# Denominators of the first batch summed on TensorE for half of the key tiles

## The chip, the cores and the metric

The kernel runs on one core of one Trainium2 chip. The metric is the device time of one execution in microseconds (us). The core has five engines that run their own instruction queues in order and wait for each other by semaphores: TensorE (PE, matrix products into PSUM; its weight loads are shown as PEld), VectorE (DVE), ScalarE (ACT), GpSimd (POOL) and SyncE (SP, which here only issues DMAs). GpSimd also issues DMAs, among them such as add what they move to what lies at the target.

## The reference

For 16 graphs of 1024 nodes with 256 features and a 0/1 adjacency matrix, two layers follow each other. The first is an attention with 8 heads of 32 features, in which queries, keys and values are the same normalized input, and the mask keeps only neighbours:

```
normed = layer_norm(x, gamma1, beta1)
qkv = normed.reshape(b, n, H, HD).transpose(0, 2, 1, 3)
scores = einsum('bhqd,bhkd->bhqk', qkv, qkv) / sqrt(HD)
attn = softmax(where(adj > 0, scores, -inf))
out = einsum('bhqk,bhkd->bhqd', attn, qkv)
x = x + out;  x = x + gelu(layer_norm(x) @ W1 + b1) @ W2 + b2
```

The second layer is a graph attention over the same mask with one score matrix per graph. Both layers get relu(layer_norm(x)) and are added to x. The change concerns only the softmax denominators of the first layer's attention, in the first of the 16 graphs ("batch 0").

## The kernel before, in words

`fast_path` writes one long program for all 16 batches without a loop on the chip. Python generators (`stream_a` to `stream_s`) yield pieces of work with a place, and the piece with the lowest place is written next. So the attention of batch b stands interleaved with the rest of batch b-1 (MLP and second layer). Only batch 0's attention has no such partner: it runs with the loading and normalization of batches 0 and 1 (`prologue`, `norm_stats` L725 to L730, `normalize` L734, L800 and L801 on GpSimd), the conversion of masks (`convert_mask` L591, fed by DMA) and some products of weights (`setup`, L675 to L700). A planner's clock and `defer` place instructions of VectorE and GpSimd some us after the work that they need, and at the end the order of each engine is fixed as written (the loop over `nc.cur_bb.bb.instructions`).

Attention is computed transposed: keys on partitions, queries along the free dimension. One *pass* takes 512 queries (`qh`) and four heads (`g`), so a batch has four passes. A pass walks over eight *tiles* of 128 keys (`kt` 0 to 7). For a tile:

- `scores` (L975) makes the four heads' scores in two PSUM tensors of 2 x 512 columns (`sc0`, `sc1`, here the *first half* and *second half*), each with one buffer. A scores tensor can thus be written only after the one before it has been read.
- The mask is added in one of two ways. TensorE multiplies it by an identity into the first half ahead of the scores (L570, `s<-mk,ident`), and ScalarE takes the exponential straight from PSUM; or VectorE adds it while it reads PSUM (L996), writes the result to SBUF, and ScalarE takes the exponential there in place (L999). In batch 0 the first half has the first way and the second half the second; in the other batches both halves have the second way.
- One tile later `weigh` (L1012) multiplies the exponentials by the values and accumulates in PSUM (`o`).

The denominator is the sum of exponentials over all keys. Sums over tiles are made elementwise, and `total` (L914) sums over partitions at the end of the pass with a product by ones (`den<-acc`). The elementwise sums are made in `acc` (the exponentials of tile 0) by GpSimd's adding DMAs (`add_up`, L1036), which read an exponential tensor from its buffer, in pool `ep` with five buffers. In batch 0 only the even tiles go this way. The odd tiles lie in pool `midp` (three buffers of a whole tile, `odd`), and VectorE adds each to the next one (L1023, `odd<-odd,odd`); `total` then multiplies both sums by ones, 4 products for `acc` and 4 for `odd`.

After that `invert` (L932, `ptds`) and `finish` (L946, `ptos`, then L948 `ot` on VectorE and L952 on GpSimd, the addition into `h`) apply the denominators. PSUM tensors of these and of most other products come from `ps_tile`, three buffers.

Of the kernel before, what the change touches and what calls it, by code (L numbers as in the profile page):

```python
# [9 lines left out]
F32 = mybir.dt.float32  # L10
# [6 lines left out]
P = 128  # L17
# [476 lines left out]
def fast_path(  # L494
# [28 lines left out]
    nc = tc.nc  # L523
    B, N, D = x.shape
    DFF = W1.shape[1]
    H, HD = 8, D // 8
    GH = 4
    NG = H // GH
# [3 lines left out]
    QW = 512  # L532
    NQH = N // QW
# [6 lines left out]
    pool = lambda name, bufs, **kw: ctx.enter_context(tc.tile_pool(name=name, bufs=bufs, **kw))  # L540
# [7 lines left out]
    midp = pool("midp", 3)  # L548
# [4 lines left out]
    smallp = pool("smallp", 3)  # L553
    psc = pool("psc", 1, space=bass.MemoryType.PSUM)
    pso = pool("pso", 1, space=bass.MemoryType.PSUM)
    psm = pool("psm", 3, space=bass.MemoryType.PSUM)

    def ps_tile(shape, name, dtype=F32):
        return psm.tile(shape, dtype, tag="ps", name=name)

# [2 lines left out]
    def matmul(out, lhsT, rhs, start=True, stop=True):  # L565
        if not quarters[0]:
            nc.tensor.matmul(out, lhsT, rhs, start=start, stop=stop)
            return
        for c in range(0, P, HD):
            nc.tensor.matmul(out[c : c + HD], lhsT[:, c : c + HD], rhs, start=start, stop=stop)  # L570
# [33 lines left out]
    ones = const.tile([P, HD], F32, name="ones")  # L604
# [58 lines left out]
    def setup():  # L663
# [8 lines left out]
        for oc in range(DC):  # L672
            pt = ps_tile([P, DC, P], f"p_wT_{oc}")
            for ic in range(DC):
                nc.tensor.transpose(pt[:, ic, :], wl[:, ic, oc * P : (oc + 1) * P], ident)  # L675
            nc.scalar.copy(wT[:, oc, :], pt.rearrange("p c q -> p (c q)"))
# [3 lines left out]
        def product(dst, lhs, rhs, n, name):  # L680

            for oc in range(DC):
                pp = ps_tile([P, n], f"p_{name}_{oc}")
                for kc in range(DC):
                    matmul(
                        pp,
                        lhs[:, kc, oc * P : (oc + 1) * P],
                        rhs[:, kc, :n],
                        start=(kc == 0),
                        stop=(kc == DC - 1),  # L690
                    )
                nc.scalar.copy(dst[:, oc, :], pp)
# [47 lines left out]
    clock = [0.0]  # L740
    deferred = []

    def defer(us, f):
        deferred.append((clock[0] + us, len(deferred), f))

        return clock[0] + us
# [149 lines left out]
    open_sums = [0]  # L896

    def make_turns():
        room = 3 - open_sums[0] - bool(summed or totalled) if open_sums[0] else 100
        while turns and turns[0][0] <= room:  # L900
            n, f = turns.pop(0)
            room -= n
            f()
# [2 lines left out]

    scored, weighed, summed, totalled = [], [], [], []

    def total(b, qh, g, os, accs):

        den = ps_tile([P, QW], f"den_{b}_{g}_{qh}")
        for j in range(GH):
            for acc in accs:
                nc.tensor.matmul(  # L914
                    den[j * HD : (j + 1) * HD, :],
                    ones,
                    acc[j // 2][:, j % 2, :],
                    start=acc is accs[0],
                    stop=acc is accs[-1],
                )  # L920
        ds = tmpp.tile([P, QW], F32, tag="w2", bufs=3, name=f"ds_{b}_{g}_{qh}")
        nc.scalar.copy(ds, den)
        totalled.append((b, qh, g, ds, os))
# [30 lines left out]
    def attention(b, st):  # L954
        va, kT = st["va"], st["kT"]

        def scores(qh, g, kt):
            qs = slice(qh * QW, (qh + 1) * QW)  # L960
            sc = [
                psc.tile([P, 2, QW], F32, tag=f"sc{i}", name=f"s_{b}_{g}_{qh}_{kt}_{i}") for i in range(2)
            ]

            by_pe = 2 if b == 0 else 0
            if by_pe:
                for j in range(by_pe):
                    matmul(
                        sc[j // 2][:, j % 2, :], ident8, st[qh][:, kt // 2, :, kt % 2], start=True, stop=False
                    )  # L970
                clock[0] += 0.45
            for j in range(GH):
                r = slice(j * HD, (j + 1) * HD)
                for c in range(0, P, P // 2):
                    nc.tensor.matmul(  # L975
                        sc[j // 2][c : c + P // 2, j % 2, :],
                        kT[r, g, kt * P + c : kt * P + c + P // 2],
                        kT[r, g, qs],
                        start=j >= by_pe,
                        stop=True,  # L980
                    )
            mb = st[qh][:, kt // 2, :, kt % 2].unsqueeze(1).to_broadcast([P, 2, QW])
            es = []
            if b == 0 and kt % 2:

                odd = midp.tile([P, 2, 2, QW], F32, tag="mid", name=f"odd_{g}_{qh}_{kt}")
            for i in range(2):
                if b == 0 and kt % 2:
                    e = odd[:, i]
                elif kt == 0:  # L990
                    e = accp.tile([P, 2, QW], F32, tag=f"acc{i}", name=f"acc_{b}_{g}_{qh}_{i}")
                else:
                    e = ep.tile([P, 2, QW], F32, tag="e", name=f"e_{b}_{g}_{qh}_{kt}_{i}")
                masked = sc[i]
                if 2 * i >= by_pe:
                    nc.vector.tensor_tensor(e, masked, mb, op=ALU.add)  # L996
                    masked = e
                es.append(e)
                weights = lambda e=e, masked=masked: nc.scalar.activation(e, masked, AF.Exp, scale=SCALE)  # L999
                if i == 0:  # L1000
                    weights()
            return es, weights

        acc = {}


        def weigh(qh, g, kt, es):
            if kt == 0:
                acc[g, qh] = pso.tile([P, QW], F32, tag="o", name=f"o_{b}_{g}_{qh}")
            o = acc[g, qh]  # L1010
            for j in range(GH):
                nc.tensor.matmul(  # L1012
                    o[j * HD : (j + 1) * HD, :],
                    va[:, kt, (g * GH + j) * HD : (g * GH + j + 1) * HD],
                    es[j // 2][:, j % 2, :],
                    start=(kt == 0),
                    stop=(kt == NT - 1),
                )
            if b == 0 and kt % 2:

                if kt > 1:
                    for n, (e, w) in enumerate(zip(es, odds[g, qh])):
                        defer(1.0 + 2.5 * n, lambda e=e, w=w: nc.vector.tensor_add(e, e, w))  # L1023
                odds[g, qh] = es
            if kt == NT - 1:
                c = tmpp.tile([P, QW], F32, tag="w2", bufs=3, name=f"os_{b}_{g}_{qh}")
                nc.vector.tensor_copy(c, o)
                weighed.append((b, qh, g, c, [s[g, qh] for s in (sums, odds) if s]))

        sums, odds = {}, {}  # L1030


        def add_up(qh, g, kt, e, i):
            if b == 0 and kt % 2:
                return
            nc.gpsimd.dma_start(sums[g, qh][i], e, accum_op=ALU.add)  # L1036

        units = [(qh, g, kt) for qh in range(NQH) for g in range(NG) for kt in range(NT)]
        for u in units:
            make_turns()  # L1040
            es, rest_of_weights = scores(*u)
            go_on()
            rest_of_weights()
            qh, g, kt = u
            if kt == 0:
                sums[g, qh] = es
            else:
                for i in range(2):
                    defer(2.0 + 1.5 * i, lambda u=u, e=es[i], i=i: add_up(*u, e, i))
            scored.append((weigh, (*u, es)))  # L1050
            yield

    def go_on():
        was_weighed, was_summed, was_totalled = weighed[:], summed[:], totalled[:]
        for l in (weighed, summed, totalled):
            l.clear()
        if scored:
            f, args = scored.pop()
            f(*args)
        summed.extend(was_weighed)  # L1060
        for args in was_summed:
            total(*args)
        for args in was_totalled:
            invert(*args)
        clock[0] += 2.0
# [354 lines left out]
    def stream_a():  # L1420
        for b in range(B):
            yield from spread(attention(b, states[b]), 32, b, b + 1)
        yield from spread(close_attention(), 4, B, B + .1)
# [55 lines left out]
    while any(p is not None for p in places):  # L1479
        i = min((p, i) for i, p in enumerate(places) if p is not None)[1]  # L1480
# [17 lines left out]
    last = {}  # L1498
# [74 lines left out]
```

## Time and profile before

| what | value |
|---|---|
| median of three runs | 3482.66 us (3480.26 to 3485.44) |
| profiled execution, span from first to last instruction | 3468.1 us |
| median of the runs above that span | 14.6 us |
| batch 0's four passes, first scores to the first scores of the next batch | about 25 to 151 us |
| TensorE busy | 3420.8 us, 99% |
| VectorE busy | 2746.2 us, 79% |
| ScalarE busy | 1858.1 us, 54% |
| GpSimd busy | 1419.9 us, 41% |

No time of the profiled execution other than its span is shown. TensorE's products are pipelined and their ends are modelled, so the time of a step is best taken from start to start. In a row of the groups the line number, the engine, the operation, what it writes and reads, shape and count come first; after the bar stand busy time and mean of one in ns; after the second bar the idle time of the engine just before such an instruction and what ended it. In a timeline a row is start, length, engine, line and operation, with the idle time before it in brackets. An instruction shown as waiting for several semaphores is put down to the one that came last.

### The profile page before, as it was taken

To read this page: it belongs to the slowest core of one execution; us is meant where nothing else is said; L and a number is where in the kernel's file an instruction comes from. 1 tells how busy PE (TensorE), PEld (TensorE's weight loads), DVE (VectorE), ACT (ScalarE), POOL (GpSimd) and SP (SyncE) were. 2 spreads that over 40 slices of the span, in tenths; PEclk is the share of its full clock that TensorE was granted. 3 is DMA by queue.
4 is the path that set the end of the run, shared out by engine and by line. 5 is a ranking of instruction groups with operands and counts; after the bars stand their busy time and mean duration, and the time that the engine had idled before them with its cause. 6 is when DMAs were issued, how large, how long until landed. Compare 5 with 4: busy or idle time off the path is not lost. (4 is left out here: it accounts for less than half of the span.)

```text
span 3468.1 us, 119040 instructions
## 1 busy us (share of the span) xinstructions
PE 3420.8 (99%) x52478; PEld 1650.4 (48%) x52478; DVE 2746.2 (79%) x5194; ACT 1858.1 (54%) x2184; POOL 1419.9 (41%) x1708
## 2 busy tenths in 40 slices
PE   6899999999999999999999999999999999999998
PEld 2244444444444444444444444444444444444477
DVE  6788788787887978878887887878878778887754
ACT  5555555555555555555555555555555555555522
POOL 4444443434434344443444434344344443434220
PEclk9999999999999999999999999999999999999999
DMA  8798989899899998989999899998999989899730
GB/s 194 147 187 172 185 162 192 180 188 191 163 187 175 189 190 165 186 169 190 193 166 189 166 189 185 180 188 168 190 177 194 188 162 184 171 193 185 147 64 14
DMA packets 281906, 598.56 MB, mean 173 GB/s; under 512 B 94882, under 2 KB 130084, under 8 KB 281380
## 3 DMA queue, kind: packets, MB, share of 16 engines
q0 software_dynamic: 124416, 453.04, 71.4%
q1 hardware_dynamic: 156676, 137.56, 15.5%
q8 instruction: 414, 6.78, 0.8%
q14 instruction: 112, 0.92, 0.1%
q10 hardware_dynamic: 288, 0.26, 0.0%
HBM read 104.21 MB, written 16.78 MB: 35 GB/s over the span
## 5 line engine op out<-in xcount | busy, mean ns | idle before, releaser
L999 ACT ACTIVATE e<-e 128x1024 f32<-128x1024 f32 x852 | 895.9, 1057 | 945.9 <-DVE e L996 704.4
L1036 POOL DMA_DIRECT2D acc<-e x864 | 759.6, 896 | 1443.4 <-DMA acc<-e 636.5
L996 DVE TENSOR_TENSOR e<-s,mk 128x1024 f32<-128x1024 f32 x852 | 1004.0, 1218 | 188.3 <-PE s L975 149.4
L975 PE MATMUL s<-kT 32*64 32x512 f32 x8192 | 579.2, 615 | 2.9 <-DVE odd L996 2.2
L1012 PE MATMUL o<-e,va 128*32 128x512 f32 x3456 | 462.3, 605 | 2.1 <-ACT e L999 2.1
L570 PE MATMUL pa<-gw,e 128*32 128x258 f32 x7648 | 453.8, 380 | 0.0
L570 PE MATMUL lg<-fT,uT 128*32 128x256 f32 x7680 | 448.6, 379 | 0.0
L570 PE MATMUL ph<-yT,w 128*32 128x256 f32 x7808 | 447.7, 379 | 0.0
L570 PE MATMUL po<-w,hid 128*32 128x256 f32 x7680 | 439.7, 379 | 0.0
L570 PEld LDWEIGHTS ph<-yT,w 128*32 128x32 f32 x7808 | 259.9, 110 | 197.5 <-issue 42.1
L570 PEld LDWEIGHTS po<-w,hid 128*32 128x32 f32 x7680 | 250.9, 110 | 208.4 <-issue 61.7
L570 PEld LDWEIGHTS lg<-fT,uT 128*32 128x32 f32 x7680 | 258.9, 110 | 189.7 <-issue 38.7
L570 PEld LDWEIGHTS pa<-gw,e 128*32 128x32 f32 x7648 | 251.6, 110 | 199.5 <-issue 48.3
L1272 ACT ACTIVATE e<-e,shift 128x512 f32<-128x512 f32 x256 | 183.2, 717 | 187.1 <-DVE e L1271 159.8
L1266 DVE SCALAR_TENSOR_TENSOR e<-lg,gw,mk 128x256 f32<-128x256 f32 x512 | 223.2, 477 | 71.6 <-PE lg L570 61.1
L1169 DVE TENSOR_TENSOR hid<-ph,b1c 128x512 f32<-128x512 f32 x256 | 175.4, 688 | 86.3 <-PE ph L570 74.8
L1012 PEld LDWEIGHTS o<-e,va 128*32 128x32 f32 x3456 | 69.0, 108 | 353.3 <-issue 221.5
L1271 DVE SCALAR_TENSOR_TENSOR e<-e 128x512 f32<-128x512 f32 x256 | 195.4, 763 | 8.8
L999 ACT ACTIVATE acc<-acc 128x1024 f32<-128x1024 f32 x124 | 131.0, 1057 | 130.4 <-DVE acc L996 125.9
L975 PEld LDWEIGHTS s<-kT 32*64 32x64 f32 x8192 | 121.2, 130 | 163.0 <-issue 106.2
L996 DVE TENSOR_TENSOR acc<-s,mk 128x1024 f32<-128x1024 f32 x124 | 146.1, 1218 | 20.9 <-PE s L975 18.4
L800 POOL TENSOR_TENSOR nrm<-nrm,g 128x256 f32<-128x256 f32 x128 | 114.0, 891 | 61.4 <-DVE nrm L734 61.4
(146 smaller groups left out, 3815.6 us busy)
## 6 DMA issues: line engine op xcount, KB each, us to landing
acc<-e POOLq DMA_DIRECT2D x864, 512.0 KB, 6.1
adj<-in_adj_dram SPq DMA_DIRECT2D x248, 256.0 KB, 5.3
h<-in_x_dram SPq DMA_DIRECT2D x64, 256.0 KB, 5.9
xb<-in_x_dram SPq DMA_DIRECT2D x128, 128.0 KB, 5.1
out_dram<-z SPq DMA_DIRECT2D x128, 128.0 KB, 3.7
adj<-in_adj_dram SPq DMA_DIRECT2D x4, 512.0 KB, 6.6
mk<-mq SPq DMA_TRANSPOSE x128, 6.4
w<-in_L_gnn_W_dram SPq DMA_DIRECT2D x2, 1024.0 KB
```

Of the source, the lines that this page charges most:

```text
L570: nc.tensor.matmul(out[c : c + HD], lhsT[:, c : c + HD], rhs, start=start, stop=stop)
L800: nc.gpsimd.tensor_mul(nrm, nrm, g1)
L975: nc.tensor.matmul(sc[j // 2][c : c + P // 2, j % 2, :], kT[r, g, kt * P + c : kt * P + c + P // 2], kT[r, g, qs], start=j >= by_pe, stop= ...
L996: nc.vector.tensor_tensor(e, masked, mb, op=ALU.add)
L999: weights = lambda e=e, masked=masked: nc.scalar.activation(e, masked, AF.Exp, scale=SCALE)
L1012: nc.tensor.matmul(o[j * HD : (j + 1) * HD, :], va[:, kt, (g * GH + j) * HD : (g * GH + j + 1) * HD], es[j // 2][:, j % 2, :], start=(kt = ...
L1036: nc.gpsimd.dma_start(sums[g, qh][i], e, accum_op=ALU.add)
L1169: nc.vector.tensor_tensor(hid[:, f0 : f0 + 2, :], ph, b1c[:, f0 : f0 + 2].unsqueeze(2).to_broadcast([P, 2, CW]), op=ALU.add,)
L1266: nc.vector.scalar_tensor_tensor(e[:, j, :], lg[:, j, :], gw[:, kt, D : D + 1], st[c // 2][:, kt // 2, qs, kt % 2], op0=ALU.add, op1=ALU.add,)
L1271: nc.vector.scalar_tensor_tensor(e, e, ALPHA, e, op0=ALU.mult, op1=ALU.max)
L1272: ready = defer(2.5, lambda: nc.scalar.activation(e, e, AF.Exp, bias=shift))
```

## The change

In batch 0, tiles 2, 4, 6 and 7 of each pass (`SUMMED_BY_PE`) are treated differently:

- Their exponentials are multiplied by ones at once, after the weighing, and accumulated in an open PSUM tensor `den` (`add_to_den`). At the end of the pass `total` adds `acc` to it. The sums on VectorE (L1023) are gone.
- Both halves of these tiles have their mask added by VectorE. TensorE's mask product is gone there. Tiles 0, 1, 3 and 5 keep both ways.
- Tiles 1, 3 and 5, not 2, 4 and 6, are now added to `acc` by DMA.
- All exponentials but those of tile 0 now lie in `ep`, with its five buffers; `odd` is gone.
- `den` has a PSUM bank of its own until the last denominator of batch 0 is made; until then `ps_tile` has two buffers, afterwards three.

The instruction order after batch 0's attention is the same in both kernels, on every engine.

```diff
-    psm = pool("psm", 3, space=bass.MemoryType.PSUM)
+    psm = pool("psm", 1, space=bass.MemoryType.PSUM)
+
+    ring = {"last": 0, "size": 2}
 
     def ps_tile(shape, name, dtype=F32):
-        return psm.tile(shape, dtype, tag="ps", name=name)
+        ring["last"] = (ring["last"] + 1) % ring["size"]
+        return psm.tile(shape, dtype, tag=f"ps{ring['last']}", name=name)
+
+    SUMMED_BY_PE = (2, 4, 6, 7)
...
-    def total(b, qh, g, os, accs):
-
-        den = ps_tile([P, QW], f"den_{b}_{g}_{qh}")
+    dens_open = {}
+
+    def add_to_den(den, es, start, stop):
         for j in range(GH):
-            for acc in accs:
-                nc.tensor.matmul(
-                    den[j * HD : (j + 1) * HD, :],
-                    ones,
-                    acc[j // 2][:, j % 2, :],
-                    start=acc is accs[0],
-                    stop=acc is accs[-1],
-                )
+            nc.tensor.matmul(
+                den[j * HD : (j + 1) * HD, :], ones, es[j // 2][:, j % 2, :], start=start, stop=stop
+            )
+
+    def total(b, qh, g, os, acc):
+
+        den = dens_open.pop((b, qh, g), None)
+        started = den is not None
+        if not started:
+            den = ps_tile([P, QW], f"den_{b}_{g}_{qh}")
+        add_to_den(den, acc, not started, True)
+        if (b, qh, g) == (0, NQH - 1, NG - 1):
+            ring["size"] = 3
...
-            by_pe = 2 if b == 0 else 0
+            by_pe = 2 if b == 0 and kt not in SUMMED_BY_PE else 0
...
-            if b == 0 and kt % 2:
-
-                odd = midp.tile([P, 2, 2, QW], F32, tag="mid", name=f"odd_{g}_{qh}_{kt}")
             for i in range(2):
-                if b == 0 and kt % 2:
-                    e = odd[:, i]
-                elif kt == 0:
+                if kt == 0:
                     e = accp.tile([P, 2, QW], F32, tag=f"acc{i}", name=f"acc_{b}_{g}_{qh}_{i}")
                 else:
                     e = ep.tile([P, 2, QW], F32, tag="e", name=f"e_{b}_{g}_{qh}_{kt}_{i}")
...
-            if b == 0 and kt % 2:
-
-                if kt > 1:
-                    for n, (e, w) in enumerate(zip(es, odds[g, qh])):
-                        defer(1.0 + 2.5 * n, lambda e=e, w=w: nc.vector.tensor_add(e, e, w))
-                odds[g, qh] = es
+            if b == 0 and kt in SUMMED_BY_PE:
+                if kt == SUMMED_BY_PE[0]:
+                    dens_open[b, qh, g] = psm.tile([P, QW], F32, tag="ps2", name=f"den_{b}_{g}_{qh}")
+                add_to_den(dens_open[b, qh, g], es, kt == SUMMED_BY_PE[0], False)
+                clock[0] += 0.85
...
         def add_up(qh, g, kt, e, i):
-            if b == 0 and kt % 2:
+            if b == 0 and kt in SUMMED_BY_PE:
                 return
             nc.gpsimd.dma_start(sums[g, qh][i], e, accum_op=ALU.add)
```

More of the change, by code (lines that the diff above doesn't have):

```diff
@@ L898, in make_turns @@
     def make_turns():
-        room = 3 - open_sums[0] - bool(summed or totalled) if open_sums[0] else 100
+        room = ring["size"] - open_sums[0] - bool(summed or totalled) if open_sums[0] else 100
         while turns and turns[0][0] <= room:
@@ L1027, in weigh @@
                 nc.vector.tensor_copy(c, o)
-                weighed.append((b, qh, g, c, [s[g, qh] for s in (sums, odds) if s]))
-        sums, odds = {}, {}
+                weighed.append((b, qh, g, c, sums[g, qh]))
+        sums = {}
         def add_up(qh, g, kt, e, i):
-            if b == 0 and kt % 2:
+            if b == 0 and kt in SUMMED_BY_PE:
                 return
```

## The prediction

> **What bounds the kernel now.** I read the page first: TensorE is busy for 99% of the span, so what counts is work that TensorE gains or loses, and stretches where it stands still. The windows view, cut at the four passes of the first batch, shows where those are. Its columns are the stretch, its length, and the busy time with the instruction count of TensorE, its weight loads, VectorE, ScalarE and GpSimd, then TensorE's granted clock, DMA share and GB/s.
>
> ```profile
> span 3468.1 us, 119040 instructions
> PE 3420.8 (99%) x52478; PEld 1650.4 (48%) x52478; DVE 2746.2 (79%) x5194; ACT 1858.1 (54%) x2184; POOL 1419.9 (41%) x1708
> ```
> ```profile
> 27.00:53.00 26.00, 24.52 (x272) 6.08 (x266) 18.42 (x26) 18.02 (x20) 11.83 (x15) 1.00 0.88 224
> 53.00:89.00 36.00, 30.12 (x450) 10.27 (x445) 29.81 (x58) 22.63 (x33) 14.78 (x18) 1.00 0.87 188
> 89.00:122.00 33.00, 32.53 (x380) 9.32 (x379) 27.58 (x44) 22.52 (x27) 19.71 (x23) 0.95 0.60 115
> 122.00:155.00 33.00, 29.30 (x348) 9.88 (x344) 23.86 (x38) 13.62 (x15) 10.95 (x13) 0.95 0.88 185
> 173.00:300.00 127.00, 126.77 (x1988) 59.07 (x1980) 102.14 (x202) 69.65 (x81) 63.74 (x77) 1.00 0.86 170
> ```
>
> From 173 us on TensorE never rests, and the order of instructions there is the same in both kernels. So whatever moves the moment at which the first batch's attention is done moves the end by as much. Before 155 us TensorE idles some 11.6 us (1.5, 5.9, 0.5 and 3.7 in the four passes), while VectorE is 71 to 84% busy. Next, TensorE's own timeline gives the prices (start, length, instruction; I take start to start):
>
> ```profile
> 48.20 0.61 PE L570 MATMUL s<-mk,ident 128*32 128x512 fp8e5 x8
> 48.75 1.11 PE L975 MATMUL s<-kT 32*64 32x512 f32 x16
> 49.79 1.06 PE L1012 MATMUL o<-e,va 128*32 128x512 f32 x8
> ...
> 59.94 1.06 PE L1012 MATMUL o<-odd,va 128*32 128x512 f32 x8
> 60.82 1.08 PE L914 MATMUL den<-acc,ones 128*32 128x512 f32 x8
> 61.68 1.08 PE L914 MATMUL den<-odd,ones 128*32 128x512 f32 x8
> ```
>
> Mask product 0.55, scores 1.04, weighing 0.88, one denominator round 0.86 us. An undisturbed tile takes 2.77 us (48.20 less 45.43): mask, scores, then ScalarE's 1.02 us on the first PSUM half, which frees it for the next mask. VectorE's instructions come from the groups (count; busy, mean ns; idle before):
>
> ```profile
> L1023 DVE TENSOR_TENSOR odd<-odd,odd 128x1024 f32<-128x1024 f32 x24 | 29.9, 1245 | 0.0
> L996 DVE TENSOR_TENSOR odd<-s,mk 128x1024 f32<-128x1024 f32 x16 | 19.5, 1220 | 8.8 <-PE s L975 8.7
> ```
>
> Back to back they start 1.14 us apart. Last I read GpSimd's timeline, since it issues the additions by DMA, and the view of that line within 26 to 180 us:
>
> ```profile
> 38.88 1.94 POOL L1036 DMA_DIRECT2D acc<-e  x2
> ...
> 104.73 2.26 POOL L952 TENSOR_TENSOR h<-h,ot 128x512 f32<-128x512 f32 x1
> 106.92 0.87 POOL L1036 DMA_DIRECT2D acc<-e  x1
> ```
> ```profile
> L1036 POOL DMA_DIRECT2D acc<-e x30: 859/877/1397, 38.9 to 178.8; - x30
> DMA to landing us min/median/max: 4.5/5.6/9.2
> ```
>
> An addition holds its source for 4.5 to 9.2 us after issue, and it is issued late where GpSimd has elementwise work ahead of it (104.73).
>
> [...] the rows show 1220 and 1245, so a mask addition costs what a sum does. [...] the trace has 5.6 with two in flight and other traffic, and I use that. [...] the trace has 0.50 from 90 to 93 us after 2.74 us of idleness.
>
> **The change part by part.** Tiles 2, 4, 6, 7 of each of the four passes are meant.
>
> *TensorE.* Removed: 16 mask products at 0.55 = 8.8 us and four closing rounds on the odd tiles, 3.4. Added: 16 rounds at 0.86 = 13.8. Net +1.6 us.
>
> *VectorE.* Removed 24 sums, added 16 mask additions: 8 x 1.22 = 9.8 us less. But the sums stood beside the chain (the next scores needed only the one mask addition), and the new additions stand in it: after scores end, the first half is free after 1.22 us, the second after 2.4, and only then can the second half of the next scores run. A step from such a tile to the next is 2.4 + 1.1 = 3.5 us, not 2.77; a step into one from a tile masked by TensorE is 2.4 to 3.0. Two such tiles of four steps gain about what they lose in a VectorE-bound stretch.
>
> *Buffers.* This decides. Odd tiles leave their own pool (three double buffers) for `ep`, which has five. It served 6 tensors per pass and now serves 14, so each buffer returns after 2.5 tiles. Half the tensors (tiles 1, 3, 5) are read by a DMA addition. Thus the write of tile 3's second half waits until tile 1's first half has landed, tile 4's first for tile 1's second, tile 5's second for tile 3's first, tile 6's first for tile 3's second, tile 7's second for tile 5's first. Behind that instruction wait all of VectorE's queue (normalization, mask conversion), behind it the next scores, and GpSimd's normalization, which stands ahead of the next DMA. At 2.5 x 2.77 = 7 us, with 1 us of exponential, issue and 5.6 us, there is no slack.
>
> Pass 1, with before's own times. GpSimd is in normalization until 38.88 in either kernel and then issues tile 1's two additions, at 38.9 and 39.6, landing after 4.7 and 6.5: 43.6 and 46.1. Tile 3's scores end at 39.4 (before 38.3: one more mask addition). Its addition waits for 43.6, ends 44.8. Tile 4's first waits for 46.1, its second ends 48.5, tile 5's scores end at 49.6 (before 44.3). Tile 3's second half is issued at 46.1 and lands after 6.3, 52.4; tile 6's additions end 54.9, tile 7's scores 56.0 (49.9). Weighing, denominator, a transpose (0.6), mask and scores: next pass's first scores 60.0, before 53.0. **+7.0 us.**
>
> Pass 2 is slower by itself (setup products; mask conversion waiting for its load), so additions land in time but for tile 7, which waits some 2 us for tile 5; VectorE's lost sums and a cold clock of before at 90 give it back. **+0.6.**
>
> Pass 3. Tile 3 waits for tile 1, which GpSimd issues after four multiplications and additions of the normalization (3.1 us): +2.7. Call X the start of VectorE's product into `ot`. GpSimd's four instructions begin about 1.1 us earlier and take 3.1, the sum into h 1.3 to 2.3, then the issue for tile 3: X+4, landing 5.2 later, X+9. Tile 5's mask addition would be due at X+4.3. Tile 6 then waits for the second half (X+12), and tile 7 for tile 5's, issued after the next four GpSimd instructions (X+13.5), landing X+18.5. Before, tile 7 stood at 112.76 with X = 101.77: X+11.0. So +7.5, less 0.5 at the pass's end: **+9.7.**
>
> Pass 4: waits of the same kind at tiles 5, 6 (1 to 3 us each) against 6 removed sums where VectorE was gapless, 141 to 160 us, and a denominator that no longer waits 2.5 us for a DMA at 127.4 (mask conversion waits beside it in both). From -4 to +4, I take **0**.
>
> Two PSUM buffers for three until the last denominator: no wait of it shows in the profile before; below no gain, above perhaps 2 us at the setup products near 66. I take 0. Sum: 7.0 + 0.6 + 9.7 + 0 = 17.3, span 3485. The median of the runs lies 14.6 us above this execution's span (3482.66 - 3468.1), which I leave as it is: **3500 us**, rounded down to 3499 since additions with less traffic beside them may land sooner.
>
> **The rivals.** A measurement of this kernel can tell about 0.2%, 7 us: same is 3475.7 to 3489.6.
> *VectorE's relief rules* (faster): it sets the end of each pass, and 9.8 us less of it come off, 3473. For: gapless from 82 to 98 and 141 to 160. Against: TensorE idles only 11.6 us in all, and the added additions are in the chain. It decides if additions landed within 3 us of their exponential, so that no buffer is waited for; the shortest was 4.5 us.
> *The waits are short* and relief, net TensorE work and longer steps cancel: +2 to +5, about 3486. For: passes 2 and 4 have slack.
> *The waits feed each other and cool TensorE*: each of some six stalls adds the doubled scores (1.1 us), and 4 us in pass 4: +28, 3511.
> *It does not do what it says*: the instruction order of the two kernels shows exactly the sums gone, and nothing moved after the first batch; excluded.
>
> **How the numbers follow.** Forecast (3490 to 3506): 0.63. Short waits 0.16; waits feeding each other 0.15; relief 0.06. The range 3483 to 3513 leaves out the relief and the outer ends of the other two. Faster 0.06, same 0.16, slower 0.78.
>
> **What would show it.** VectorE's mask addition waiting for the DMA line, some 15 us in all before 190 us; tile 3's mask addition of pass 1 starting near 43.6; 16 rounds on `e` into `den`; TensorE's continuous work beginning some 17 us after 173; clock at 0.5 in the stalls. It is wrong if those waits total under 5 us, or if VectorE's waits pass without TensorE standing still.

## The result and the profile after

| | median | lowest to highest |
|---|---|---|
| kernel before | 3481.46 us (4 runs) | 3475.96 to 3485.44 |
| changed kernel | 3517.72 us (4 runs) | 3511.15 to 3523.14 |

The ratio is 1.0114, 95% interval 1.0094 to 1.0133. By the medians the change costs some 36 us, by the ratio 40 (33 to 46). That is twice the 17 us that were forecast, or more, and the median lies above the range of 3483 to 3513.

The page of the changed kernel begins with its span and the busy times. TensorE is busy for 98% of a longer span. Its busy time has grown by 21.4 us and its idle time by 22.6 us. Since its net work was put at +1.6 us, busy time can't be read as work alone here; a part of it is the lower clock that is spoken of further down.

```profile
span 3512.1 us, 119006 instructions
PE 3442.2 (98%) x52446; PEld 1660.2 (47%) x52446; DVE 2739.9 (78%) x5186; ACT 1860.2 (53%) x2184; POOL 1417.9 (40%) x1708
```

The windows of the changed kernel have the same columns as those of before (stretch, length, busy time of TensorE, weight loads, VectorE, ScalarE, GpSimd, then granted clock, DMA share, GB/s). The first four are cut where those of before were.

```profile
27.00:53.00 26.00, 21.37 (x192) 5.18 (x184) 13.71 (x22) 13.49 (x15) 11.80 (x15) 0.93 0.83 214
53.00:89.00 36.00, 33.84 (x460) 11.48 (x448) 25.37 (x47) 21.54 (x33) 9.46 (x12) 1.00 0.93 186
89.00:122.00 33.00, 29.37 (x296) 9.07 (x294) 21.25 (x44) 18.97 (x23) 17.12 (x22) 0.95 0.51 99
122.00:155.00 33.00, 29.94 (x288) 8.61 (x284) 20.22 (x34) 17.49 (x19) 9.59 (x12) 0.86 0.72 140
...
180.00:190.00 10.00, 8.39 (x108) 2.31 (x95) 6.59 (x9) 8.95 (x9) 3.50 (x6) 1.00 0.83 157
190.00:300.00 110.00, 109.77 (x1720) 50.87 (x1716) 87.53 (x176) 58.97 (x66) 54.44 (x66) 1.00 0.90 174
```

VectorE does less in each of the first four (13.71 us for 18.42 in the first) and TensorE waits all the same. TensorE's continuous work begins between 180 and 190 us, not at 173. So far this is the forecast. TensorE's clock is lower too: the share not granted, times the length, adds up to 8.1 us in these four windows (26 x 0.07 + 33 x 0.05 + 33 x 0.14) and to 3.3 us in those of before. By this estimate at most some 5 us of the first batch's delay are slower products and not idle time.

**Where the first batch loses.** VectorE's timeline of the changed kernel shows the mask additions of pass 1 and pass 3, each with the idle time before it and what ended that.

```profile
43.95 1.23 DVE L1001 TENSOR_TENSOR e<-s,mk 128x1024 f32<-128x1024 f32 x1 [5.43 <-DMA acc<-e]
46.54 2.36 DVE L1001 TENSOR_TENSOR e<-s,mk 128x1024 f32<-128x1024 f32 x2 [1.36 <-DMA acc<-e]
...
109.79 1.22 DVE L1001 TENSOR_TENSOR e<-s,mk 128x1024 f32<-128x1024 f32 x1 [4.53 <-DMA acc<-e]
...
113.73 2.36 DVE L1001 TENSOR_TENSOR e<-s,mk 128x1024 f32<-128x1024 f32 x2 [1.39 <-DMA acc<-e]
...
120.47 1.23 DVE L1001 TENSOR_TENSOR e<-s,mk 128x1024 f32<-128x1024 f32 x1 [3.10 <-DMA acc<-e]
```

The releaser is the addition by DMA that still reads the buffer. The view of that DMA line (L1040, L1036 before) within 26 to 200 us adds up who waited for it:

```profile
L1040 POOL DMA_DIRECT2D acc<-e x31: 861/875/1184, 39.1 to 199.0; - x31
...
who waited for it (us, times):
  DVE e L1001: 26.0, 13
  POOL acc L1040: 10.6, 5
...
DMA to landing us min/median/max: 4.5/5.9/9.4
```

The wait of VectorE did not exist before: the same view of L1036 names no instruction of VectorE. Further, one addition waits for another into the same half of `acc`: the first of pass 1 is issued at 39.08 us and lands after 4.8, and GpSimd stands 3.34 us (`<-DMA acc<-e`) before it issues the third at 44.36. Such waits come to 10.6 us in 5 places, and they are not new: within the same 26 to 200 us it was 10.2 us in 7 places before.

To measure the delay I set the same products of both traces against each other, the weighing of the second tile of each pass (`o<-acc`), which occurs once per pass:

| pass | before, us | after, us | later by |
|---|---|---|---|
| 1 | 31.3 | 31.6 | 0.2 |
| 2 | 55.7 | 64.5 | 8.8 |
| 3 | 91.5 | 99.4 | 7.9 |
| 4 | 118.8 | 136.7 | 17.9 |
| batch 1, first | 156.2 | 176.5 | 20.2 |
| batch 1, second | 206.4 | 223.8 | 17.4 |

The later weighings, up to 360 us of the kernel before, are as late. The first batch explains 17.4 us and no more.

**Where the rest is lost.** The view of waits on TensorE, from 230 us to the end, has one row in the changed kernel that counts (us in total, times, longest):

```profile
PE pf L575 <- DVE z L1317: 16.0, 14, 1.1
PE den L918 <- DMA acc<-e: 1.1, 1, 1.1
```

Nothing in the kernel before waits like that; its largest sums there are 0.9 us. TensorE's timeline near one of the 14 places, changed kernel first, then before at the same last two products:

```profile
386.02 1.93 PE L575 MATMUL pa<-gw,e 128*32 128x258 f32 x32
387.88 0.66 PE L1146 MATMUL pty<-ident,y 128*128 128x128 f32 x4
...
390.39 1.04 PE L918 MATMUL den<-acc,ones 128*32 128x512 f32 x8
391.25 1.93 PE L575 MATMUL pa<-gw,e 128*32 128x258 f32 x32
394.32 1.07 PE L575 MATMUL pf<-wo,fT 128*32 128x256 f32 x16 [1.15 <-DVE z L1317]
```
```profile
373.80 1.93 PE L570 MATMUL pa<-gw,e 128*32 128x258 f32 x32
375.54 1.05 PE L570 MATMUL pf<-wo,fT 128*32 128x256 f32 x16
```

From `pa` to `pf` it is 3.07 us start to start, where it was 1.74. VectorE's timeline at the same place, again changed kernel first, says what `pf` waits for: the last reading of that same `pa`, which can only start when `pa` is complete (391.25 + 1.93 = 393.18) and ends at 394.17. In the kernel before that reading ends at 376.72, and `pf` has begun at 375.54.

```profile
393.25 0.16 DVE L1313 COPY dens<-pa 128x1 f32<-128x1 f32 x1 [1.27 <-PE pa L575]
...
393.69 0.48 DVE L1317 SCALAR_TENSOR_TENSOR z<-pa,l,z 128x256 f32<-128x256 f32 x1
```
```profile
376.24 0.48 DVE L1313 SCALAR_TENSOR_TENSOR z<-pa,l,z 128x256 f32<-128x256 f32 x1
```

`pf` does not use `pa`. It waits because it is to be written into the PSUM buffer that `pa` holds. In the changed kernel three tags with one buffer each are handed out in strict turn, also after the first batch. The order at the end of each batch is that of the rows above: `pa` of tile 6 is begun, `pty` and `den` of the next batch are written, `pa` is completed, and `pf` of tile 7 follows. By turn `pf` is the third after `pa` and gets its buffer, just filled. In the kernel before, `ps_tile` takes three buffers of one pool, and the order of products is the same. There `pf` begins 1.18 us ahead of the end of the last reading of `pa`, at each of the 14 places, so it lies in another buffer; in the changed kernel it begins 0.15 us after that end, at all 14. How the pool chose its buffer is not shown. Each wait makes all later products 1.35 us later in the comparison of products, and 14 x 1.35 = 18.9.

The sum is 3481.46 + 17.4 + 18.9 = 3517.8 us, against 3517.72 measured. That it fits so closely is chance: the interval leaves room for over 6 us either way. Between the two profiled executions the difference grows to 43.9 us at the last products. The 7.5 us above 17.4 + 18.9 are small steps at other places, and they belong to the execution of before that was profiled, one of its quicker ones: set against the same execution, the kernel with both delays taken out (below) falls back by as much, from 1.6 us ahead at 206 us to 5.9 behind at the end.

### The profile page after: what moved, and what is told of

Its sections match the earlier page's. It is cut to its first block, busy times and chain, and to the rows that moved or that the text cites. A ratio compares the mean times of both kernels' runs of the same rounds, so it can differ in the third digit from the quotient of the medians.

```text
span 3512.1 us, 119006 instructions
## 1 busy us (share of the span) xinstructions
PE 3442.2 (98%) x52446; PEld 1660.2 (47%) x52446; DVE 2739.9 (78%) x5186; ACT 1860.2 (53%) x2184; POOL 1417.9 (40%) x1708
## 5 line engine op out<-in xcount | busy, mean ns | idle before, releaser
L1004 ACT ACTIVATE e<-e 128x1024 f32<-128x1024 f32 x884 | 929.9, 1057 | 1012.4 <-DVE e L1001 817.9
L1040 POOL DMA_DIRECT2D acc<-e x864 | 759.5, 896 | 1474.8 <-DMA acc<-e 634.3
L1001 DVE TENSOR_TENSOR e<-s,mk 128x1024 f32<-128x1024 f32 x884 | 1041.8, 1218 | 238.4 <-PE s L985 173.5
L985 PE MATMUL s<-kT 32*64 32x512 f32 x8192 | 592.6, 617 | 9.7 <-DVE e L1001 8.4
L1017 PE MATMUL o<-e,va 128*32 128x512 f32 x3584 | 483.4, 608 | 1.6 <-ACT e L1004 1.6
L575 PEld LDWEIGHTS pa<-gw,e 128*32 128x32 f32 x7648 | 258.7, 110 | 195.1 <-issue 45.3
L575 PE MATMUL pf<-wo,fT 128*32 128x256 f32 x1920 | 127.0, 380 | 16.2 <-DVE z L1317 16.0
```

The lines of the kernel that those rows point to most:

```text
L985: nc.tensor.matmul(sc[j // 2][c : c + P // 2, j % 2, :], kT[r, g, kt * P + c : kt * P + c + P // 2], kT[r, g, qs], start=j >= by_pe, stop= ...
L1017: nc.tensor.matmul(o[j * HD : (j + 1) * HD, :], va[:, kt, (g * GH + j) * HD : (g * GH + j + 1) * HD], es[j // 2][:, j % 2, :], start=(kt = ...
```

## The experiments

The two causes can be taken out one by one. Each experiment was timed beside the kernel before: the first four beside 3478.95 us (15 runs, 3472.40 to 3486.42), the last four beside 3476.11 us (53 runs, 3466.89 to 3489.85).

**The turn of buffers alone, in the kernel before.**

```diff
-    psm = pool("psm", 3, space=bass.MemoryType.PSUM)
+    psm = pool("psm", 1, space=bass.MemoryType.PSUM)
+    ring = {"last": 0, "size": 3}
     def ps_tile(shape, name, dtype=F32):
-        return psm.tile(shape, dtype, tag="ps", name=name)
+        ring["last"] = (ring["last"] + 1) % ring["size"]
+        return psm.tile(shape, dtype, tag=f"ps{ring['last']}", name=name)
```

> The kernel before with one edit: its pool of three PSUM buffers is replaced by three tags of one buffer each, taken in strict turn, from the start. Theory R (rotation): a product takes the buffer of a tensor that VectorE has not yet read; TensorE waits some 1.15 us once in each of 14 batches, the first batch stays as it is: 16 to 26 us longer, 3498 to 3508. Theory E (only the exponentials' five buffers cost time): no change, 3478 to 3486.

Measured: 3500.11 us (3493.56 to 3505.85), ratio 1.0055 (1.0036 to 1.0074). The waits of TensorE from 230 us on show the same row, to the digit:

```profile
PE pf L573 <- DVE z L1316: 16.0, 14, 1.1
```

The first batch is that of before (second pass at 55.9 us, third at 91.4, fourth at 118.3). So this part, which has nothing to do with the denominators of the first batch, costs some 19 us by itself (0.55% of 3479, 13 to 26 by the interval).

**The changed kernel with the pool of three.** `den` comes from the same pool. The planner still counts two buffers in the first batch (`ring["size"]`), as in the changed kernel.

```diff
-    psm = pool("psm", 1, space=bass.MemoryType.PSUM)
+    psm = pool("psm", 3, space=bass.MemoryType.PSUM)
...
-        ring["last"] = (ring["last"] + 1) % ring["size"]
-        return psm.tile(shape, dtype, tag=f"ps{ring['last']}", name=name)
+        return psm.tile(shape, dtype, tag="ps", name=name)
...
-                    dens_open[b, qh, g] = psm.tile([P, QW], F32, tag="ps2", name=f"den_{b}_{g}_{qh}")
+                    dens_open[b, qh, g] = ps_tile([P, QW], f"den_{b}_{g}_{qh}")
```

> The changed kernel with one edit: PSUM tensors come from one pool of three again, and the open denominators of the first batch from that pool too. The order of instructions is the changed kernel's on every engine. Theory R: the first batch still ends 17 us late, and nothing is added afterwards: 3497 to 3501. Theory E: no difference to the changed kernel, about 3518.

Measured: 3496.89 us (3493.55 to 3505.46), ratio 1.0049 (1.0032 to 1.0066). The row of `pf` waiting for `z` is gone from TensorE's waits. VectorE's waits from 26 to 200 us keep theirs:

```profile
DVE e L1000 <- DMA acc<-e: 30.5, 13, 5.4
```

So the first batch alone costs about 17 us (0.49% of 3479, 11 to 23 by the interval), the size forecast.

**The changed kernel with its own buffers for tiles 1, 3 and 5.** The exponentials that the DMA reads lie in `midp` again, in whole-tile buffers; the strict turn stays.

```diff
+            if b == 0 and kt in (1, 3, 5):
+                odd = midp.tile([P, 2, 2, QW], F32, tag="mid", name=f"odd_{g}_{qh}_{kt}")
             for i in range(2):
-                if kt == 0:
+                if b == 0 and kt in (1, 3, 5):
+                    e = odd[:, i]
+                elif kt == 0:
```

> The changed kernel with one edit: the exponentials of tiles 1, 3 and 5, which DMAs add, lie in the whole-tile buffers of before, not in the five of ep. Theory E and the prediction's walk: VectorE's waits for landed additions (26 us in all) vanish, the first batch ends within 5 us of before, so 12 to 20 us less than the changed kernel: 3498 to 3506. If the longer step of tiles masked by VectorE were the cause, less than 5 us would come back: above 3512.

Measured: 3497.15 us (3492.52 to 3501.23), ratio 1.0057 (1.0040 to 1.0073). VectorE's waits for the adding DMA are gone, and the first batch is back: the second weighing of batch 1 stands at 205.1 us, 206.4 before. What is left is the other cause:

```profile
PE pf L575 <- DVE z L1321: 16.0, 14, 1.1
```

**Both taken out.** The edits of the last two experiments together.

> Both edits, the pool of three and the whole-tile buffers for tiles 1, 3 and 5. If the two causes are independent and complete, the two losses vanish together: 3478 to 3488. Above 3492 a third cause is left.

Measured: 3477.57 us (3475.53 to 3489.43, 12 runs), ratio 0.9999 (0.9988 to 1.0010). Without the two delays the changed kernel takes the time of the kernel before. What else the change does in the first batch stays in this version: the sums on TensorE, the masks by VectorE, the planner's count of two PSUM buffers. Together they cost nothing that the interval of 0.1% tells. The two costs add: 0.49% for the first batch alone and 0.55 or 0.57% for the turn alone make 1.04 to 1.06%, and both at once measured 1.14 (0.94 to 1.33).

**One buffer per batch.** Is it the strict turn as such, or the one tensor that meets a full buffer? On top of the own buffers for tiles 1, 3 and 5, the last `pf` of each batch steps on by two and thus gets the buffer of `pty`.

```diff
-        ring["last"] = (ring["last"] + 1) % ring["size"]
+        step = 2 if name.startswith("pf_") and name.endswith("_7") else 1
+        ring["last"] = (ring["last"] + step) % ring["size"]
```

> The changed kernel with the exponentials of tiles 1, 3 and 5 in their own pool again, and the three PSUM buffers in strict turn, as the change has it, except that one tile in each batch, the last `pf`, steps on by two. It thereby gets the buffer of the transposes `pty`, as in the kernel before, and not that of the `pa` before it, which VectorE has yet to read. Theory (this one buffer is the whole of what the turn costs): the wait of `pf` for z, 16.0 us in 14 places, is gone, and the time is that of the kernel before, 3475 to 3482 us, a ratio of 0.998 to 1.002. Rival (a strict turn costs by itself, and another tile will wait in the place of this one): waits of about 1 us per batch stand elsewhere, and the time stays near 3497, ratio 1.005.

Measured: 3477.46 us (3471.56 to 3484.56, 14 runs), ratio 0.9997 (0.9988 to 1.0006). The longest rows of TensorE's waits from 230 us on:

```profile
PE puT L576 <- ACT gw L1257: 1.6, 3, 0.9
PE den L919 <- DMA acc<-e: 1.2, 2, 0.8
PE pf L576 <- DVE yT L1155: 1.1, 1, 1.1
```

The 14 waits are gone and no wait of once per batch takes their place. The whole second cause is one tensor per batch, in one of three buffers.

**The sums on TensorE alone.** Both delays out, and the masks of tiles 2, 4, 6 and 7 added as before, one half by TensorE.

```diff
-            by_pe = 2 if b == 0 and kt not in SUMMED_BY_PE else 0
+            by_pe = 2 if b == 0 else 0
```

> Both delays taken out (exponentials of tiles 1, 3, 5 in their own pool, PSUM buffers from one pool of three), and the masks of tiles 2, 4, 6 and 7 added by TensorE as before, so that of the announced change the sums on TensorE alone are left. TensorE gets 16 mask products at 0.55 us back, 8.8 us, and VectorE loses 16 additions of 1.22 us, 19.5 us. Theory (in the first batch the chain of scores, mask and exponential sets the step, and TensorE's product is cheaper in it than VectorE's two additions, but TensorE's own time rises): the two cancel, 3474 to 3482 us, within 0.2% of the kernel with both delays out. Rival one (VectorE's relief, the prediction's faster rival): the first batch ends 7 to 10 us earlier, 3468 to 3471. Rival two (TensorE bounds the first batch too): 8.8 us later, 3486.

Measured: 3478.16 us (3468.26 to 3485.47, 22 runs), ratio 1.0002 (0.9993 to 1.0010). Neither relief nor burden: VectorE's busy time falls to 2714.7 us, from 2746.2 before, and TensorE gets its products back, but the second weighing of batch 1 stands at 204.4 us, 204.8 in the kernel with both delays out.

**The masks alone.** The kernel before with whole masks by VectorE on those tiles, its sums kept.

```diff
-            by_pe = 2 if b == 0 else 0
+            by_pe = 2 if b == 0 and kt not in (2, 4, 6, 7) else 0
```

> The kernel before with one part of the change alone: the masks of tiles 2, 4, 6 and 7 of the first batch added wholly by VectorE, the sums on VectorE kept. TensorE loses 16 products of 0.55 us (8.8 us); VectorE gains 16 additions of 1.22 us (19.5 us), each in the chain from scores to exponential. Theory (with its sums kept VectorE is the bound of those passes, 71 to 84% busy before): the first batch ends 8 to 15 us later, 3488 to 3495 us. Rival (TensorE's saving pays for it, the additions stand in VectorE's idle time): 3474 to 3482 us, no difference.

Measured: 3482.73 us (3476.18 to 3492.85, 20 runs), ratio 1.0019 (1.0009 to 1.0030), 6.6 us: a loss that the interval tells from none, but smaller than the 8 to 15 us of the theory. In the trace the second weighing of batch 1 is at 214.0 us, 7.6 late. TensorE waits within 26 to 230 us for VectorE's additions:

```profile
PE s L975 <- DVE odd L996: 4.5, 4, 2.8
PE s L570 <- DVE e L996: 4.2, 5, 1.8
```

In the kernel before the first of these is 2.2 us in 2 places, and the second is not among the largest. So 16 mask additions cost the kernel some 7 us when its 24 sums stay, and nothing that can be told when they go (0.9999 with them, 1.0002 without). Taking the sums away pays for the mask additions and earns nothing more that these runs show.

**Earlier issue of the adding DMAs.** The changed kernel with the pool of three, in whose first batch an addition enters GpSimd's queue 0.1 us after its exponential.

```diff
-                    defer(2.0 + 1.5 * i, lambda u=u, e=es[i], i=i: add_up(*u, e, i))
+                    defer((0.1 if b == 0 else 2.0) + (0.1 if b == 0 else 1.5) * i, lambda u=u, e=es[i], i=i: add_up(*u, e, i))
```

> The changed kernel with the PSUM buffers from one pool of three (so that only the delay of the first batch is left), in whose first batch the additions by DMA are put into GpSimd's queue 0.1 us after their exponential, not 2.0 and 3.5, and so ahead of some of the normalization and of the sum into h. Theory (part of the wait is late issue behind GpSimd's elementwise work): VectorE's waits for the additions in the first batch fall from 30.5 us to 10 to 18, and the time from 3497 to 3484 to 3491. Rival (what counts is the landing, 4.5 us and more after issue; or an issue that stands early waits for its exponential and holds GpSimd's normalization back): 3493 to 3500, waits of 25 us and more.

Measured: 3492.42 us (3487.92 to 3497.31, 6 runs), ratio 1.0045 (1.0030 to 1.0061); with the later issue it was 1.0049 (1.0032 to 1.0066). It falls between what the two theories expected, and the intervals overlap, so a gain is not shown. The view of the DMA line:

```profile
L1039 POOL DMA_DIRECT2D acc<-e x30: 854/886/1258, 39.4 to 198.0; - x30
...
  DVE e L1000: 24.8, 11
  POOL acc L1039: 9.2, 4
...
DMA to landing us min/median/max: 4.5/6.2/9.4
```

VectorE's waits fall by 5.7 us only. In pass 1 the first addition is issued at 39.4 us, for 39.1 without the edit: GpSimd's normalization still stands ahead of it. The third, at 44.68 us, waits 3.32 us for the one before it into the same half of `acc`. For the most part it is then not the place in the queue that holds the buffers. How the rest divides between landing, the waits of additions for each other and the normalization stays open. A sixth buffer in `ep` was not tried.

## Why the prediction was wrong

**What held.** The step called *Buffers* was right in mechanism, and its sum in size. Tile 3's mask addition of pass 1 was put at 43.6 us and starts at 43.95. By the table above the passes lost 8.5, -0.9, 10.0 and 2.3 us and the stretch after them -2.8, where 7.0, 0.6, 9.7 and 0 (from -4 to +4) were worked out: 17.2 with the signs, and 17.4 with what pass 1 begins late, for 17.3. The runs agree: the changed kernel with only this delay left took 17 us more than before, and with its own buffers for tiles 1, 3 and 5 the first batch was back. That the sum is met to 0.1 us is luck: single passes are off by up to 2.3 us and cancel with the stretch after them, and the lower clock, up to some 5 us by the estimate above, had its place in a rival and not in the sum. VectorE waited 26.0 us rather than some 15. TensorE's own waits for VectorE's mask additions, within 26 to 180 us, come to 13.8 us (7.9 for the second halves, 5.9 for the first), for 2.9 before. TensorE's new rounds on `e` are the forecast sixteen, as a row of the groups of the changed kernel shows (26 to 200 us; 128 instructions of 8 per round):

```profile
L918 PE MATMUL den<-e,ones 128*32 128x512 f32 x128 | 19.1, 621 | 0.0
```

The doubled scores after a stall are there as well. TensorE's timeline of the changed kernel has one after 2.57 us of waiting, and the window that follows has the granted clock at 0.50; from these scores to the weighing it is 2.48 us, not 1.04.

```profile
151.48 0.61 PE L575 MATMUL s<-mk,ident 128*32 128x512 fp8e5 x8 [2.57 <-DVE e L1001]
152.02 2.55 PE L985 MATMUL s<-kT 32*64 32x512 f32 x16
154.50 1.83 PE L1017 MATMUL o<-e,va 128*32 128x512 f32 x8
```
```profile
154.00:156.00 2.00, 2.00 (x12) 0.40 (x12) 0.61 (x3) 0.56 (x1) 1.23 (x2) 0.50 0.96 165
```

In the kernel before, the scores at 89.56 us, which follow 2.74 us of waiting and a mask product, took 1.92 us to the weighing, and the granted clock from 90 to 93 us was 0.50.

The step *VectorE* was right that the additions removed and added about balance: with both delays out the ratio is 0.9999. The experiment with the sums alone (1.0002, 0.9993 to 1.0010) rules out a relief of 7 to 10 us even without the added masks, and the one with the masks alone shows what the sums pay for.

**What failed.** Two sentences of the prediction carry the error. The first: two PSUM buffers for three cause "no wait", "I take 0". It looked only at the number of buffers, and only until the last denominator of the first batch. For that stretch the 0 was right: the kernel with its own buffers for tiles 1, 3 and 5 has two PSUM buffers there, in turn, and its second weighing of batch 1 stands at 205.1 us, not later than 206.4. But the diff also replaces the rule by which `ps_tile` hands them out, and this rule holds to the end of the kernel. The measured price is 14 x 1.35 = 18.9 us in the trace and 19 to 20 us in the two runs that have this delay alone, with 0 put in its place. The second: from 173 us on "the order of instructions there is the same in both kernels", so that what moves the end of the first batch "moves the end by as much". The order is indeed the same. But order is not all that binds TensorE: which buffer each tensor lies in adds dependencies that no list of instructions shows. The same error sits in the rival that was excluded because "nothing moved after the first batch".

The trace of before had what was needed to see it. TensorE's rows at 373.80 and 375.54 show `pf` directly behind the completed `pa`, and VectorE's row at 376.24 the reading that comes later; with three buffers in turn, and two other tensors taken since `pa` was begun, `pf` must meet `pa` unread. The changed kernel does rotate through three buffers; its 14 waits, 16.0 us in all, show that here a rotation in order of allocation does not let a product begin beside the last reading of a tensor that stays open while two others come and go.

**The 14.6 us** that were left between the span and the median are settled: a run takes its span plus 1.8 us (3513.9 and 3512.1 for the changed kernel), which makes 3469.9 us of the profiled span, and the rest is the spread of the kernel before, whose 53 runs reach from 3466.89 to 3489.85 us. Adding the delay to the median was right.

**The rivals.** *The waits feed each other and cool TensorE* named 3511 us, nearest to the result, but for another reason: the cooler clock is there (0.86 from 122 to 155 us, for 0.95 before), and yet the first batch lost 17.4 us and not 28. *The waits are short* and *VectorE's relief* are excluded by the kernel with the pool of three, 0.49% slower, and by the two kernels without delays, which are not faster.

No version here beats the kernel before: the three without the delays stand at 0.9997, 0.9999 and 1.0002.

## What to carry to other kernels

A change to how buffers are handed out is a change to every later tensor from that pool: list which tensor follows which in each buffer, and look for one that is taken soon after a tensor that stayed open long. Where TensorE is otherwise gapless, a wait of 1 us per batch passes unseen in the page (98% busy for 99%) and shows only when waits are added up by pair of lines. When a tensor moves to another pool, count how long each reader holds it, the slowest one first; here it was a DMA, with a median of 5.9 us from issue to landing.

## What was not expected of the hardware

In four traces (before, changed kernel, changed with the pool of three, and that with the earlier issue), within 26 to 200 us, an addition by DMA of 512 KB landed at the earliest 4.5 us after its issue, in the median after 5.5 to 6.2 and at the latest after 9.2 to 9.4. So long it held its source: the first of pass 1 in the changed kernel lands at 43.9 us (39.08 + 4.8), and the mask addition that waits for its buffer starts at 43.95.

The prediction was rounded down by 1 us because additions might land sooner with less traffic beside them. Within the trace of before the two go together: in the 4.5 us after issue the core's DMAs, the additions among them, moved 120 to 168 GB/s for the seven additions that landed within 4.8 us (issued from 38.9 to 173.7 us), and 165 to 276 for six that took 7.5 to 9.2 us (65.4 to 152.3). Between the kernels it did not show: within 26 to 200 us the changed kernel moved 154 GB/s for 172, and its median landing was 5.9 us for 5.5.

In these traces TensorE, which hardly rests after the first batch (109.77 us busy of 110 from 190 us on, changed kernel), passes a single wait of 1.15 us on in full, and with a surcharge: every product after it is 1.35 us later. The rows of `pa` and `pf` above show the rest: in the kernel before, `pf` starts 0.19 us ahead of the end of `pa` as the trace models it (373.80 + 1.93 = 375.73, against 375.54), and after this wait that overlap is not there: 1.15 + 0.19 = 1.34.
